# A two-layer vision block on one core: other bands for the second image's convolution, and w_out's tiles seeded and evicted by ScalarE

## The chip, the cores and the metric

The kernel runs on one core of a Trainium2 chip. The metric is the device time of one execution in microseconds. TensorE (PE) multiplies matrices and writes PSUM; VectorE (DVE), ScalarE (ACT) and GpSimd (POOL) work on elements; SyncE (SP) and GpSimd issue DMAs. Each engine runs its own instruction stream in the order in which the program issued it, and the streams meet at semaphores.

## The reference

The input is x of shape (2, 56, 56, 384), in fp32. Layer 0 is neighbourhood attention (12 heads, 7 x 7) and an MLP of 1536 hidden channels. Layer 1 is where the change lies:

```python
h = _layernorm(x, n1_g, n1_b)
p = h @ w_in + b_in                              # 384 -> 768 channels
local = conv 3x3, depthwise, "SAME" (p, k_conv)
lr, rl = _ema_scan(local, axis=2), _ema_scan(local, axis=2, reverse=True)
tb, bt = _ema_scan(local, axis=1), _ema_scan(local, axis=1, reverse=True)
mixed = 0.25 * (lr + rl + tb + bt) + local
mixed = _layernorm(mixed, on_g, on_b)
x = x + (mixed @ w_out + b_out)                  # 768 -> 384
h2 = _layernorm(x, n2_g, n2_b)
return x + gelu(h2 @ w1 + b1) @ w2 + b2          # 384 -> 1536 -> 384
```

An EMA scan is y[t] = 0.6 y[t-1] + 0.4 x[t] along one axis.

## The kernel before

Tokens (pixels) go in groups of four tiles of 128. In time order: attention up to about 600 us; layer 0's MLP, for some groups in a form with seven products for a 2 x 2 block product ("by seven"), for groups g = 5 to 12 in plain form; then layer 1's out projection and MLP, groups ("dgroups") 0 to 2 in plain form up to 1915.6 us, and the rest by seven (the "tail").

A plain group runs 12 hidden blocks m (w1: two times three matmuls each into a bank of PSUM, and GELU by ScalarE, L1208) and then four tiles k of w2 (`tokens`, L1215: 24 matmuls of 384 columns). A layer-0 group is followed by `project_in` of its tokens (w_in), which stores p to DRAM (p_d).

**The convolution beside the matmuls.** Its work is cut into jobs: a `Band` is one image, one block of 128 channels (of six) and a range of rows from BANDS. For one Band: load p's rows (pt), the centre tap (`centre`, on ScalarE if the job is loaded ahead, L1287, else on VectorE, L1289), eight more taps on VectorE (L1304), a scan along the rows both ways (`both_ways`, L1250 to L1254), a product on ScalarE (L1319), and stores of loc and of both to DRAM. When an image's bands are done, `Columns` jobs, one for each block of channels, read loc back turned (`line`, four copies on ScalarE for a half, L1352), scan along the columns, scale the result into "mixed" (L1370, four on ScalarE for a half) and add it to mix_d in DRAM by a DMA that POOL issues (L1323). Band 2 of the second image cannot start before its rows of p are in DRAM.

The steps of these jobs are dealt into the program by class `Beside`: each piece of TensorE work calls `beside.go(worth, own)`, which raises a debt by rate x worth less what VectorE has of its own there, and then issues steps, each with an estimated cost (`us`, and the values yielded by `both_ways`), until the debt is paid. `until(name)` issues all that is left up to a job. So each engine's order is fixed when the program is built: a ScalarE copy that belongs to a Band stands in ScalarE's stream wherever the dealer put it.

**The out projection.** `load_mix(g)` loads a dgroup's "mixed" (mx), and `measure_beside` transposes it (xi, L1440) during m = 3, 5, 7, 9 of the group before, for VectorE's statistics (L221); at m = 10 `close` makes rs, the reciprocal deviation. `project_out(g + 1)` then comes between the 12 blocks of w1 and the four tiles of w2 of group g, four tiles of 12 matmuls; VectorE evicts each with one instruction, product x rs + x (L1485):

```python
nc.vector.scalar_tensor_tensor(
    x3[:, k, :], ps, inner.rs[:, k : k + 1], x[:, k, :], ALU.mult, ALU.add
)
```

`project_out(0)` comes behind the last layer-0 tile of w2, and ahead of it stand that tile's statistics (`norm_w.add`, `close_by_pool`) and `xn = normalized(norm_w, x2, ...)` (four ScalarE instructions, L257). The w2 tiles of a dgroup are seeded: `seeded(res, k)` copies the residual into the PSUM bank by ScalarE (L1225), the matmuls add to it, and ScalarE copies the sum out (L2019). Two seeds are issued before the first w2 tile, each further one after an eviction. `bank()` gives the banks y and y_end in turn; each third tile of the projection takes one of the three banks named pt.

**The switch** to the tail lies in dgroup 2, at k = 2 of w2: `beside.until((1, NI - 1))` ends the convolution, its SBUF pool is closed, the tail's pool is opened in the same space, and VectorE makes sums of w1 and w2 (L1602, L1692). After the last tile POOL makes sums of the tail's input (xsums, L1615).

Of the kernel before, what the change touches and what calls it, by code (L numbers as in the profile page):

```python
# [33 lines left out]
F32 = mybir.dt.float32  # L34
# [27 lines left out]
DECAY, GAIN = 0.6, 0.4  # L62
BANDS = (
    ((0, 28), (28, 47), (47, 56)),
    ((0, 27), (27, 45), (45, 56)),
)
HALF = H // 2
QUARTER = 14
# [45 lines left out]
class Beside:  # L114
# [2 lines left out]

    def __init__(self):
        self.jobs, self.due, self.finished, self.idle = [], 0.0, set(), True
        self.late, self.rate, self.begun = [], 1.04, False  # L120
        self.steps = self.run()

    def behind(self, kind=object):
# [55 lines left out]
def block_kernel(ctx: ExitStack, tc: tile.TileContext, ins: dict, out: bass.AP):  # L179
# [28 lines left out]
    class Norm:  # L208
# [7 lines left out]
        def add(self, k, parts):  # L216

            n = parts[0].shape[0]
            st = self.small.tile([P, 2, 6], F32, name="st")
            for i, x in enumerate(parts):  # L220
                nc.vector.bn_stats(st[:n, i, :], x)  # L221
            nc.vector.bn_aggr(self.mv[:n, k, :], st[:n, : len(parts), :])

        def close(self, k, n=P, first=0):
            rs = self.rs[:n, first:k]
# [868 lines left out]
    def passes(xs, xn, w1, w2, between=lambda ps: None):  # L1094
# [145 lines left out]
        def half(name, tag, bufs=2):  # L1240
            return cp.tile([P, HALF, W], F32, name=name, tag=tag, bufs=bufs)

        def us(lines, each=1.04):

            return 0.2 + lines * W * each / 1000.0

        def both_ways(dst, src):
            n = dst.shape[1]
            d = decay[:, : n * W]
            nc.vector.tensor_tensor_scan(flat(dst), d, flat(src), 0.0, ALU.mult, ALU.add)  # L1250
            end = dst[:, :, W - 1 :]
            nc.vector.scalar_tensor_tensor(end, end, tail - 1.0, end, ALU.mult, ALU.add)
            yield us(n, 2.2) + 0.2
            nc.vector.tensor_tensor_scan(  # L1254
                flat(dst)[:, ::-1], d, flat(dst)[:, ::-1], 0.0, ALU.mult, ALU.add
            )
            yield us(n, 2.2)

        class Band:

# [64 lines left out]
        class Columns:  # L1325
# [32 lines left out]
            def steps(self):  # L1358
# [16 lines left out]
                for c in range(2):  # L1375
                    t = self.lines[c]
                    for step, took in enumerate(both_ways(t, t)):
                        if self.b == 0 and c == step == 0:
                            for h in range(2):
                                mixed.append(half("mixed", "out", 4))  # L1380
                                nc.sync.dma_start(out=flat(mixed[h]), in_=self.rows(mix_d, h))
                        if self.b == 1 and c == 0 and step == 1:
                            self.turn(nc.scalar.copy)
                        yield took
                        if c == 1 and step == 0:
                            behind = beside.behind()
                    for h in range(2):
                        if self.b == 0:
                            to = mixed[h][:, :, c * HALF : (c + 1) * HALF]
                            nc.vector.scalar_tensor_tensor(  # L1390
                                to, t[:, :, h * HALF : (h + 1) * HALF]
                                .rearrange("p w h -> p h w"), share, to, ALU.mult, ALU.add,
                            )
                            if c == 0:
                                self.turn(nc.scalar.copy, (h,))
                            elif h == 1 and isinstance(behind, Columns):
                                behind.turn(nc.scalar.copy, (0,))
                            yield us(HALF / 2, 2.0)
                        else:
                            beside.later(lambda c=c, h=h: turn_back(c, h), 3.0 + 3.5 * c)  # L1400
                    if c == 0:
                        beside.behind()
# [58 lines left out]
        def measure_beside(m, g, ahead):  # L1461


            n = dgroups[g][1]
            k = m // 2 - (1 if g else 2)
            if m == 4:
                add_row(ahead[1], n, "b_out")
            if m == 10 and g:
                ahead[2].close(n)
            if m % 2 == 1 and 0 <= k < n:  # L1470
                measure(ahead[0], ahead[2], k)
                return 2 * STATS
            return 0.0

        def project_out(g, mx, x, inner, then=None):
            n = dgroups[g][1]
            x3 = io.tile([P, NT, C], F32, name="xc")
            norm = Norm(sm)
            for k in range(n):
                third = then is None and k % 3 == 2  # L1480
                ps = tokens(
                    [mx[:, c, :] for c in range(NI)], w_out, k,
                    ps_t.tile([P, C], F32, name="y", tag="pt") if third else None,
                )
                nc.vector.scalar_tensor_tensor(  # L1485
                    x3[:, k, :], ps, inner.rs[:, k : k + 1], x[:, k, :], ALU.mult, ALU.add
                )
                norm.add(k, [x3[:, k, :]])
                if then is not None:
                    then(k)  # L1490
                beside.go(OUT, 2 * STATS)
            norm.close(n)
            return x3, norm
# [108 lines left out]
                engine.tensor_tensor(to, x, y, ALU.subtract)  # L1602
            return *sums, t4, other

        def sums_of_input(hT):

            a, b = slice(0, MT // 2), slice(MT // 2, MT)
            t = tp.tile([P, 4, MT // 2], F32, name="xsums", bufs=1)
            for to, x, y, op in (
                (t[:, 0], hT[:, 0, b], hT[:, 1, b], ALU.add),  # L1610
                (t[:, 1], t[:, 0], hT[:, 0, a], ALU.subtract),
                (t[:, 2], hT[:, 0, a], hT[:, 0, b], ALU.subtract),
                (t[:, 3], hT[:, 1, a], t[:, 1], ALU.subtract),
            ):
                nc.gpsimd.tensor_tensor(to, x, y, op)  # L1615
            return t

        def hidden_by_seven(hT, xsums, w1, w1_sums, s12, measuring, b1):
# [176 lines left out]
        for g, (t0, n) in enumerate(groups):  # L1795
# [19 lines left out]
            if g == last:  # L1815
                beside.until((0, NI - 1))
                load_row(0, "b2_1")
                ahead = load_mix(0)
                beside.rate = 1.06
            if g < last:  # L1820
                x_next, n_next = xs.pop(g + 1), groups[g + 1][1]
                norm_next = Norm(sm) if g < EARLY.stop else Ready(g + 1)
# [89 lines left out]
            if g < last:  # L1912
                add_row(x_next, n_next, "b2_0")
            if g == last:
                ahead[2].close(dgroups[0][1])
                w1, w2_1, w_parts = weights(1)
                for part in w_parts[:3]:
                    part()
# [68 lines left out]
        for g, (t0, n) in enumerate(dgroups[:switch]):  # L1987
# [10 lines left out]
            ahead = load_mix(g + 2)  # L1998
            seeds = [seeded(res, k) for k in range(2)]
            for k in range(n):  # L2000
                if g == switch - 1 and k == 2:

                    beside.until((1, NI - 1))
                    cctx.close()
                    tp = pctx.enter_context(tc.tile_pool(name="tail", bufs=1, reuse_waits="tile"))
                    w1_sums = more_of_w1(w1, three, nc.vector)
                    w2_sums, sum_steps = sums_of_w2(w2, nc.vector)
                if k == n - 1:
                    hT = channels(xn, dgroups[g + 1][1], *n2)
                ps = tokens(hid, w2, k, onto=seeds.pop(0))  # L2010
# [12 lines left out]

        bctx.close()
        ps_y, ps_u, bank_b, banks_b = open_banks(pctx, "tail")
        ps_m = ps_u
        xsums = sums_of_input(hT)
        for step in sum_steps:  # L2030
            step()
        for g, (t0, n) in enumerate(dgroups):
# [136 lines left out]
```

## Time and profile before

| what | value |
|---|---|
| median of 3 runs | 2568.47 us (2565.06 to 2572.3) |
| the profiled execution | 2569.35 us, span 2567.6 us |
| granted TensorE clock, mean | 0.997 |
| TensorE busy | 2532.3 us (99%) |
| VectorE busy | 1986.1 us (77%) |
| ScalarE busy | 1124.0 us (44%) |
| GpSimd busy | 570.3 us (22%) |

The table gives the busy time of each engine over the whole span. Since stages differ, a wait is read in its place: in the windows of the span, in the list of waits, and in the timeline of each engine around it.

### The profile page before, as it was taken

Reading aid. Unit: us, or ns where it says so; the run is one execution under the profiler, and the core shown is the slowest. Engines: PE = TensorE matmul, PEld = TensorE weight load, DVE = VectorE, ACT = ScalarE, POOL = GpSimd, SP = SyncE. Lnnn points to the kernel's source line nnn. Section 1 sums busy time; section 2 is a strip of 40 time slices with the busy share of each in tenths; the row PEclk is TensorE's granted clock in tenths of the full one; section 3 lists DMA queues with packets and bytes.
Section 4 is the critical chain, followed back from the end, with each engine's and each line's share of the span. In section 5 each row is a group of like instructions: output and inputs, shape, how many; then the busy total and the mean of one; then the engine's idle time right before and its main releaser. Section 6 shows DMA issues by size and latency. Waiting matters only on the chain. (4 is left out here: it accounts for less than half of the span.)

```text
span 2567.6 us, 41855 instructions
## 1 busy us (share of the span) xinstructions
PE 2532.3 (99%) x16676; PEld 1733.0 (67%) x16678; DVE 1986.1 (77%) x3715; ACT 1124.0 (44%) x2033; POOL 570.3 (22%) x618
## 2 busy tenths in 40 slices
PE   9999999999999999999999999999999999999999
PEld 5666666666698887455545555554568888888888
DVE  3888878887554453899999996999877877878862
ACT  4656555555443444334555343332862233233222
POOL 0111111111542331010110101011123333333332
PEclk9999999999999999999999999999999999999999
DMA  7432454225522223557687667667781333333210
GB/s 220 152 99 91 148 190 152 90 83 193 168 61 84 68 68 91 167 159 213 179 237 266 214 191 220 202 185 185 203 197 24 75 74 74 74 75 74 47 28 21
DMA packets 155596, 342.96 MB, mean 134 GB/s; under 512 B 11158, under 2 KB 109696, under 8 KB 153088
## 3 DMA queue, kind: packets, MB, share of 16 engines
q1 hardware_dynamic: 124096, 255.65, 29.4%
q0 software_dynamic: 26352, 57.81, 13.3%
q10 hardware_dynamic: 4944, 26.74, 3.0%
q8 instruction: 133, 2.18, 0.4%
q14 instruction: 71, 0.58, 0.1%
HBM read 176.39 MB, written 134.88 MB: 121 GB/s over the span
## 5 line engine op out<-in xcount | busy, mean ns | idle before, releaser
L1304 DVE SCALAR_TENSOR_TENSOR loc<-pt,taps,loc 128x1045 f32<-128x1045 f32 (+17 forms) x288 | 370.6, 1287 | 16.4 <-ACT loc L1287 8.3
L1197 PE MATMUL mm<-hT,w 128*128 128x512 f32 x720 | 319.6, 599 | 0.1
L573 ACT ACTIVATE pts<-pts 119x448 f32<-119x448 f32 (+5 forms) x396 | 210.7, 573 | 107.4 <-DVE pts L563 103.1
L563 DVE TENSOR_TENSOR pts<-sc,bias 119x448 f32<-119x448 f32 (+5 forms) x396 | 219.1, 615 | 45.3 <-PE sc L552 45.0
L1197 PEld LDWEIGHTS mm<-hT,w 128*128 128x128 f32 x720 | 136.0, 192 | 163.0 <-issue 157.6
L1180 DVE STREAM_TRANSPOSE hT<-xn 32x96 f32<-32x96 f32 x784 | 211.3, 269 | 27.7 <-ACT xn L257 17.5
L406 PE MATMUL ps<-hT,wqkv 128*128 128x448 f32 x504 | 206.5, 554 | 2.1 <-ACT vs L451 1.5
L1452 DVE STREAM_TRANSPOSE turned<-mx 32x192 f32<-32x192 f32 x528 | 194.9, 369 | 8.6 <-issue 1.7
L1215 PE MATMUL y_end<-w,hid 128*128 128x384 f32 x552 | 181.9, 486 | 1.4 <-ACT y_end L1225 1.4
L1215 PE MATMUL y<-w,hid 128*128 128x384 f32 x552 | 181.9, 486 | 0.0
L1215 PEld LDWEIGHTS y_end<-w,hid 128*128 128x128 f32 x552 | 104.6, 190 | 73.8 <-ACT y_end L1225 1.7
L1208 ACT ACTIVATE hid<-mm,chan 128x512 f32<-128x512 f32 x120 | 82.1, 685 | 163.4 <-PE mm L1197 163.4
L1215 PEld LDWEIGHTS y<-w,hid 128*128 128x128 f32 x552 | 104.3, 190 | 71.3 <-issue 0.5
L406 PEld LDWEIGHTS ps<-hT,wqkv 128*128 128x128 f32 x504 | 92.0, 191 | 85.3 <-issue 75.5
L1197 PE MATMUL mm<-hT,w_in 128*128 128x512 f32 x324 | 141.9, 596 | 0.6 <-DVE hid_u L1653 0.6
L229 POOL TENSOR_TENSOR rs<-rs,mhalf 128x4 f32<-128x4 f32 (+4 forms) x60 | 57.2, 953 | 312.0 <-DVE rs L226 310.9
L1634 PE MATMUL ua<-hT,w 128*128 128x256 f32 x504 | 122.5, 379 | 0.0
L552 PEld LDWEIGHTS sc<-qT,kT 32*100 32x100 f32 (+3 forms) x3168 | 87.8, 169 | 46.7 <-DVE sum L582 7.6
L1323 POOL DMA_DIRECT2D mix_d<-both x36 | 31.8, 883 | 377.9 <-ACT both L1319 245.8
L592 PE MATMUL o<-pts,vt 100*32 100x112 f32 (+3 forms) x3168 | 115.1, 262 | 0.5 <-ACT pts L573 0.5
L1197 PEld LDWEIGHTS mm<-hT,w_in 128*128 128x128 f32 x324 | 61.7, 192 | 78.3 <-issue 73.3
L1641 ACT ACTIVATE hid<-hid_u,chan 128x256 f32<-128x256 f32 x168 | 76.1, 500 | 82.1 <-DVE hid_u L1653 67.8
(207 smaller groups left out, 4977.6 us busy)
## 6 DMA issues: line engine op xcount, KB each, us to landing
loc<-loc_d SPq DMA_DIRECT2D x24, 784.0 KB
xa<-x_d SPq DMA_DIRECT2D x24, 768.0 KB
xa<-rows POOLq DMA_DIRECT2D x24, 768.0 KB, 11.8
bias<-in_bias_t ACTq DMA_DIRECT2D x13, 1344.0 KB
p_d<-mx SPq DMA_DIRECT2D x11, 1536.0 KB
mx<-mix_d SPq DMA_DIRECT2D x11, 1536.0 KB
v_d<-vs SPq DMA_DIRECT2D x49, 192.0 KB
xr<-in_x SPq DMA_DIRECT2D x49, 192.0 KB
```

The source lines that it names most:

```text
L406: nc.tensor.matmul(ps, lhsT=wqkv[:, c, m * P : (m + 1) * P], rhs=hT[:, c, half_of(n)], start=c == 0, stop=c == NC - 1,)
L552: nc.tensor.matmul(sc[i // 2][: w.keys, i % 2, q : q + TT], lhsT=kT[d, hg, w.keys_at + r * w.kc : w.keys_at + (r + w.rows) * w.kc], rhs=qT ...
L563: nc.vector.tensor_tensor(self.pts[:n, h : h + 2, lo:hi, :], sc[half][:n, :, at * TT : (at + hi - lo) * TT].rearrange("p h (c q) -> p h c ...
L573: nc.scalar.activation(t, t, AF.Exp)
L592: nc.tensor.matmul(o[i * HD : (i + 1) * HD, self.slot, :TT], lhsT=w.vt[:n, c, h * HD : (h + 1) * HD], rhs=self.pts[:n, i, c, :], start=c = ...
L1180: nc.vector.transpose(hT[j : j + HD, :, k * P + i : k * P + i + HD], xn[i : i + HD, k, :].rearrange("p (c q) -> p c q", c=NC)[:, :, j : j ...
L1197: nc.tensor.matmul(ps[:, : n * P], lhsT=w[:, c, m * P : (m + 1) * P], rhs=hT[:, c, : n * P], start=c == 0, stop=c == NC - 1,)
L1208: nc.scalar.activation(t[:, : n * P], ps[:, : n * P], AF.Gelu, bias=col(b1, m))
L1215: nc.tensor.matmul(ps, lhsT=t[:, k * P : (k + 1) * P], rhs=w[:, m, :], start=m == 0 and onto is None, stop=m == len(lhs) - 1, skip_group_c ...
L1304: nc.vector.scalar_tensor_tensor(to, pt[:, lo + dy - self.top : hi + dy - self.top, xt : xt + n], self.tap(dy, dx), to, ALU.mult, ALU.add,)
L1452: nc.vector.transpose(t[j : j + HD].rearrange("p (m c) -> p m c", m=NI)[:, :, i : i + HD], mx[i : i + HD, :, k * P + j : k * P + j + HD],)
L1634: nc.tensor.matmul(bank[:, i, :], lhsT=w[:, m * P : (m + 1) * P], rhs=x, start=start and i == 0, stop=True, skip_group_check=True,)
```

## The change

The second image's bands become 27, 9 and 20 rows instead of 27, 18 and 11. The dealer's estimates become a fixed 0.25 us plus a part by elements, with other values for the scans, and its rate falls from 1.04 to 1.0, and from 1.06 to 0.97 from the last layer-0 group on. For projections of dgroups 0 to 3 (`then is None`) the norm is closed by `close_both_ways`, which also makes sd, the deviation (a further POOL instruction); tiles k = 0, 1 and 3 are seeded with x * sd by ScalarE, the matmuls add to that, and ScalarE evicts with a product by rs, so that rs * (x * sd + product) stands in the place of product * rs + x. Tile 2 stays on VectorE. Two seeds are issued ahead of the projection, the third after tile 0's eviction. The end of the convolution, the closing of its pool and the sums of w1 and w2 move from k = 2 of dgroup 2 to behind its last tile; xsums move from POOL to VectorE, the sums of w2 from VectorE to POOL. The matmuls, the taps' and scans' numbers and the DMAs' kinds stay.

```diff
--- before.py
+++ after.py
@@ -62,7 +62,7 @@
 DECAY, GAIN = 0.6, 0.4
 BANDS = (
     ((0, 28), (28, 47), (47, 56)),
-    ((0, 27), (27, 45), (45, 56)),
+    ((0, 27), (27, 36), (36, 56)),
 )
 HALF = H // 2
 QUARTER = 14
@@ -117,7 +117,7 @@
 
     def __init__(self):
         self.jobs, self.due, self.finished, self.idle = [], 0.0, set(), True
-        self.late, self.rate, self.begun = [], 1.04, False
+        self.late, self.rate, self.begun = [], 1.0, False
         self.steps = self.run()
 
     def behind(self, kind=object):
@@ -220,6 +220,14 @@
             for i, x in enumerate(parts):
                 nc.vector.bn_stats(st[:n, i, :], x)
             nc.vector.bn_aggr(self.mv[:n, k, :], st[:n, : len(parts), :])
+
+        def close_both_ways(self, k):
+
+            self.sd = self.small.tile([P, NT], F32, name="sd")
+            rs, sd = self.rs[:, :k], self.sd[:, :k]
+            nc.vector.scalar_tensor_tensor(sd, self.mv[:, :k, 1], EPS, ones[:, :k], ALU.add, ALU.mult)
+            nc.gpsimd.tensor_tensor(rs, sd, mhalf[:, :k], ALU.pow)
+            nc.gpsimd.tensor_tensor(sd, sd, rs, ALU.mult)
 
         def close(self, k, n=P, first=0):
             rs = self.rs[:n, first:k]
@@ -1240,9 +1248,9 @@
         def half(name, tag, bufs=2):
             return cp.tile([P, HALF, W], F32, name=name, tag=tag, bufs=bufs)
 
-        def us(lines, each=1.04):
-
-            return 0.2 + lines * W * each / 1000.0
+        def us(lines, each=1.04, fixed=0.25):
+
+            return fixed + lines * W * each / 1000.0
 
         def both_ways(dst, src):
             n = dst.shape[1]
@@ -1250,11 +1258,11 @@
             nc.vector.tensor_tensor_scan(flat(dst), d, flat(src), 0.0, ALU.mult, ALU.add)
             end = dst[:, :, W - 1 :]
             nc.vector.scalar_tensor_tensor(end, end, tail - 1.0, end, ALU.mult, ALU.add)
-            yield us(n, 2.2) + 0.2
+            yield us(n, 2.18)
             nc.vector.tensor_tensor_scan(
                 flat(dst)[:, ::-1], d, flat(dst)[:, ::-1], 0.0, ALU.mult, ALU.add
             )
-            yield us(n, 2.2)
+            yield us(n, 2.18, 0.03)
 
         class Band:
 
@@ -1395,7 +1403,7 @@
                                 self.turn(nc.scalar.copy, (h,))
                             elif h == 1 and isinstance(behind, Columns):
                                 behind.turn(nc.scalar.copy, (0,))
-                            yield us(HALF / 2, 2.0)
+                            yield us(HALF / 2, 2.0, 0.0)
                         else:
                             beside.later(lambda c=c, h=h: turn_back(c, h), 3.0 + 3.5 * c)
                     if c == 0:
@@ -1466,7 +1474,7 @@
             if m == 4:
                 add_row(ahead[1], n, "b_out")
             if m == 10 and g:
-                ahead[2].close(n)
+                ahead[2].close_both_ways(n)
             if m % 2 == 1 and 0 <= k < n:
                 measure(ahead[0], ahead[2], k)
                 return 2 * STATS
@@ -1476,12 +1484,26 @@
             n = dgroups[g][1]
             x3 = io.tile([P, NT, C], F32, name="xc")
             norm = Norm(sm)
+            lhs, seeds = [mx[:, c, :] for c in range(NI)], []
+
+            def seed(k):
+                ps = bank()
+                nc.scalar.mul(ps, x[:, k, :], inner.sd[:, k : k + 1])
+                return ps
+
+            if then is None:
+                seeds = [seed(k) for k in range(2)]
             for k in range(n):
-                third = then is None and k % 3 == 2
-                ps = tokens(
-                    [mx[:, c, :] for c in range(NI)], w_out, k,
-                    ps_t.tile([P, C], F32, name="y", tag="pt") if third else None,
-                )
+                if then is None and k != 2:
+                    ps = tokens(lhs, w_out, k, onto=seeds.pop(0))
+                    nc.scalar.mul(x3[:, k, :], ps, inner.rs[:, k : k + 1])
+                    if k == 0 and n > 3:
+                        seeds.append(seed(3))
+                    norm.add(k, [x3[:, k, :]])
+                    beside.go(OUT, STATS)
+                    continue
+                third = ps_t.tile([P, C], F32, name="y", tag="pt") if then is None else None
+                ps = tokens(lhs, w_out, k, third)
                 nc.vector.scalar_tensor_tensor(
                     x3[:, k, :], ps, inner.rs[:, k : k + 1], x[:, k, :], ALU.mult, ALU.add
                 )
@@ -1602,7 +1624,7 @@
                 engine.tensor_tensor(to, x, y, ALU.subtract)
             return *sums, t4, other
 
-        def sums_of_input(hT):
+        def sums_of_input(hT, engine=nc.gpsimd):
 
             a, b = slice(0, MT // 2), slice(MT // 2, MT)
             t = tp.tile([P, 4, MT // 2], F32, name="xsums", bufs=1)
@@ -1612,7 +1634,7 @@
                 (t[:, 2], hT[:, 0, a], hT[:, 0, b], ALU.subtract),
                 (t[:, 3], hT[:, 1, a], t[:, 1], ALU.subtract),
             ):
-                nc.gpsimd.tensor_tensor(to, x, y, op)
+                engine.tensor_tensor(to, x, y, op)
             return t
 
         def hidden_by_seven(hT, xsums, w1, w1_sums, s12, measuring, b1):
@@ -1816,7 +1838,7 @@
                 beside.until((0, NI - 1))
                 load_row(0, "b2_1")
                 ahead = load_mix(0)
-                beside.rate = 1.06
+                beside.rate = 0.97
             if g < last:
                 x_next, n_next = xs.pop(g + 1), groups[g + 1][1]
                 norm_next = Norm(sm) if g < EARLY.stop else Ready(g + 1)
@@ -1912,7 +1934,7 @@
             if g < last:
                 add_row(x_next, n_next, "b2_0")
             if g == last:
-                ahead[2].close(dgroups[0][1])
+                ahead[2].close_both_ways(dgroups[0][1])
                 w1, w2_1, w_parts = weights(1)
                 for part in w_parts[:3]:
                     part()
@@ -1998,13 +2020,6 @@
             ahead = load_mix(g + 2)
             seeds = [seeded(res, k) for k in range(2)]
             for k in range(n):
-                if g == switch - 1 and k == 2:
-
-                    beside.until((1, NI - 1))
-                    cctx.close()
-                    tp = pctx.enter_context(tc.tile_pool(name="tail", bufs=1, reuse_waits="tile"))
-                    w1_sums = more_of_w1(w1, three, nc.vector)
-                    w2_sums, sum_steps = sums_of_w2(w2, nc.vector)
                 if k == n - 1:
                     hT = channels(xn, dgroups[g + 1][1], *n2)
                 ps = tokens(hid, w2, k, onto=seeds.pop(0))
@@ -2023,10 +2038,15 @@
 
 
 
+        beside.until((1, NI - 1))
+        cctx.close()
+        tp = pctx.enter_context(tc.tile_pool(name="tail", bufs=1, reuse_waits="tile"))
         bctx.close()
         ps_y, ps_u, bank_b, banks_b = open_banks(pctx, "tail")
         ps_m = ps_u
-        xsums = sums_of_input(hT)
+        xsums = sums_of_input(hT, nc.vector)
+        w1_sums = more_of_w1(w1, three, nc.vector)
+        w2_sums, sum_steps = sums_of_w2(w2)
         for step in sum_steps:
             step()
         for g, (t0, n) in enumerate(dgroups):
```

## The prediction

> **What bounds the kernel now.** I read the page's busy line first, then the table of stages in windows of 20 us, then the waits of TensorE, then the timelines around each wait.
>
> ```profile
> PE 2532.3 (99%) x16676; PEld 1733.0 (67%) x16678; DVE 1986.1 (77%) x3715; ACT 1124.0 (44%) x2033; POOL 570.3 (22%) x618
> ```
>
> TensorE is busy 99% of the span, so the time is its work plus its gaps. The change leaves its matmuls alone: it can only close gaps, open gaps, or alter the granted clock. The windows (columns: length, PE, PEld, DVE, ACT, POOL busy with counts, granted clock, DMA share, GB/s) say where gaps are:
>
> ```profile
> 1600.00:1620.00 20.00, 20.00 (x64) 11.79 (x63) 14.25 (x15) 2.95 (x5) 0.00 (x0) 1.00 0.33 108
> 1620.00:1640.00 20.00, 16.02 (x55) 9.42 (x54) 19.37 (x26) 5.80 (x8) 2.14 (x3) 0.98 0.45 155
> ...
> 1740.00:1760.00 20.00, 16.78 (x47) 7.70 (x45) 19.30 (x23) 7.20 (x11) 3.18 (x3) 0.97 0.70 160
> 1760.00:1780.00 20.00, 19.05 (x51) 9.31 (x52) 19.17 (x32) 4.73 (x7) 2.50 (x2) 0.86 0.40 133
> 1840.00:1860.00 20.00, 17.44 (x47) 8.20 (x46) 17.92 (x16) 12.38 (x19) 1.75 (x2) 0.91 0.90 210
> ```
>
> Ahead of 1620 PE is full; then come short gaps, with the clock down after them. TensorE's waits from 1600 to 2000 name their owners (total, times, longest):
>
> ```profile
> PE xi L1440 <- DVE st L221: 6.7, 2, 4.2
> PE tp L271 <- DVE xc L1485: 2.5, 1, 2.5
> PE y L1215 <- DVE xc L1485: 1.5, 1, 1.5
> PE y_end L1215 <- ACT y_end L1225: 1.4, 1, 1.4
> ```
>
> That is 12.1 us in all, 10.7 of it owed by VectorE. Why VectorE is late stands in its timeline (start, duration, ..., idle before and its releaser):
>
> ```profile
> 1584.03 0.14 DVE L226 SCALAR_TENSOR_TENSOR rs<-mv,ones 128x4 f32<-128x4 f32 x1
> 1605.40 0.74 DVE L1289 TENSOR_SCALAR loc<-pt,taps 128x1008 f32<-128x1008 f32 x1 [21.23 <-DMA pt<-p_d]
> ```
>
> It stood 21.23 us for image 2's second band, whose rows had not landed, and from then on runs after a schedule it has lost. The gaps end in a slow clock:
>
> ```profile
> 1847.33 0.68 PE L1440 MATMUL xi<-ident,mx 128*128 128x128 f32 x3 [2.56 <-DVE st L221]
> 1847.81 6.92 PE L1197 MATMUL mm<-hT,w 128*128 128x512 f32 x12
> 1855.22 5.32 PE L1197 MATMUL mm<-hT,w 128*128 128x512 f32 x12
> ```
>
> The same 12 matmuls take 6.92 us after a gap of 2.56 and 5.32 us otherwise: 1.6 us lost on top. After the 4.17 us gap at 1760.95 they take 7.33, 2.0 lost; after the 2.48 us gap 36 matmuls take 16.68 where 15.6 is usual, 1.1 lost; after 1.5 us, 0.1. Removable in all: 12.1 + 1.6 + 2.0 + 1.1 + 0.2 = **17 us**.
>
> **The change part by part.**
>
> *Bands, rate, estimates.* A second band of 9 rows needs fewer tokens of project_in, so the 21 us stand goes; what is left between bands is a store and a load, some 2 to 4 us, with no TensorE instruction behind it. The taps, scans and DMAs stay the same in kind: a 504-element tap is about 0.75 us and a 1120-element one 1.41 (line through 616 elements 0.86 and 1008 elements 1.27). The count is the same, 8 taps and two scans for each of three bands. The lower rate pushes the last steps to the last plain tile. I credit this part with all 17 us; bound on the other side: nothing, if VectorE stays late. I take 17, since VectorE's lateness starts at one place and the reason is removed; it also loses 12 evictions of 0.62 us (L1485).
>
> *Seeds and evictions on ScalarE.* In four projections, tiles 0, 1 and 3 get a seed x*sd written to PSUM by ScalarE and are evicted by it. The form is not in the trace; nearest rows are xn L257 (2.50 for four, 0.62 each) and the copy of a seed L1225 (0.48). 0.6 each, 24 of them, 14.4 us on an engine 44% busy: no cost as work. The cost is in the place. An engine's instructions run in program order, so the first matmul of w_out now waits for all that is emitted on ScalarE ahead of its seed. Before, it waited for nothing.
>
> Weighed against that, the Trainium skill ("ScalarE: Activation LUTs", Rules for kernel authors) sends add and mul to VectorE, up to three times faster in bf16. Here, fp32 from PSUM, the rows say 0.62 on both (L257, L1485). By the rule the seeds and evictions would cost ScalarE more than they spare VectorE, and each first seed would come 1.2 us later than by the row (some 5 us more over four projections). I keep the row.
>
> (A) Projection 0 follows the last layer-0 tile of w2. ScalarE first has that tile's normalization, whose chain the trace has, spread over time because VectorE was late:
>
> ```profile
> 1611.57 7.58 PE L1215 MATMUL y_end<-w,hid 128*128 128x384 f32 x23
> ...
> 1619.19 0.48 ACT L1946 COPY xc<-y_end 128x384 f32<-128x384 f32 x1 [6.22 <-PE y_end L1215]
> ...
> 1630.55 0.55 DVE L221 BATCH_NORM_STATS2 st<-xc 128x6 f32<-128x384 f32 x1
> ...
> 1631.68 1.01 POOL L238 TENSOR_TENSOR rs<-rs,mhalf 128x4 f32<-128x4 f32 x1 [43.80 <-DVE off L237]
> ...
> 1633.00 2.50 ACT L257 ACTIVATE xn<-xc,sh,rs 128x384 f32<-128x384 f32 x4 [13.33 <-POOL sh L239]
> ```
>
> From the end of the matmul: eviction 0.04 + 0.48, statistics to POOL 1631.68 - 1630.55 = 1.13 (and 0.1 to get there), POOL to xn 1.32, xn 2.50, seed 0.62 + 0.06 to TensorE: 6.25, and half a tap step in front of the statistics, 0.5: **6.75 us**, in a place where TensorE had no gap. (If VectorE were as late as in this trace, 11 us more: the upper end.)
>
> (B) Projections 1 and 2 follow the last w1 pair. Ahead of the seed: GELU of the last group (0.2 + 0.59) and the centre tap of 1120 elements (1.12 for 1008, so 1.2), then 0.6: **2.6 us each**. Projection 3 has two sets of line copies there, and the trace shows these nearly as they will stand:
>
> ```profile
> 1864.39 3.07 ACT L1352 COPY line<-loc 128x392 f32<-128x392 f32 x4
> 1867.25 0.66 ACT L1208 ACTIVATE hid<-mm,chan 128x512 f32<-128x512 f32 x1
> 1867.81 3.10 ACT L1352 COPY line<-loc 128x392 f32<-128x392 f32 x4
> ...
> 1866.18 4.03 PE L1215 MATMUL y_end<-w_out,mx 128*128 128x384 f32 x12
> ```
>
> ScalarE is done with these at 1870.8, TensorE starts w_out at 1866.18: with 0.62 for the seed, **5.2 us**.
>
> (C) From w_out's last tile to w2. The w2 seed (L1225) came early because VectorE evicted; now it stands behind ScalarE's eviction of tile 3 (0.2 + 0.6), a product of 1120 elements (1.0 to 1.1) and its own 0.48 + 0.06: **2.4 us** in groups 0 and 1; in group 2 four line copies (3.0) instead: **4.35 us**.
>
> *The norm's sd chain.* One more POOL product of 0.20 (as sh L239) behind rs 1.03: done by the seed unless VectorE is 2 us late. Zero, range 0 to 2.
>
> (D) *The switch.* The scans now end in the last plain tile. From the start S of w_out's first tile: w_out 15.5, gap 4.35, w2 31.0, transposes 1.5, so the plain part ends at S + 52.4. VectorE's remaining scans follow ScalarE's line copies (3.0 each) and end about S + 51.5; then mixed x4 (3.15) and its two stores by POOL. Copies into the tail's tiles that lie where "mixed" lay wait for these to land: 8.9 us from issue to landing around the switch (9.6 over the stage). Issue at S + 54.7, landing S + 63.6, copy 0.58, against S + 58.9 when TensorE needs it: **5.3 us**; 3 to 8 by landings of 6.7 to 11.8; 0 if the scans end 5 us sooner. In the trace of before these stores left at 1907.26, 8.4 us before the tail began, and nothing waited. Moving xsums to VectorE costs four short operations (768 elements 0.95; 256 about 0.4) and is hidden behind TensorE's first uz; the w2 sums on POOL (768 elements about 2.2, so 1152 about 3.3, four: 13) have 20 us until they are used.
>
> *Sum.* 6.75 + 2 x 2.6 + 5.2 + 2 x 2.4 + 4.35 + 5.3 = 31.6 us of new gaps. Clock after them, by the rows above: 2.0 for each of A, B3, C3, D, 1.4 for each B of 2.6, 1.1 for each C of 2.4: 13. The Trainium skill ("TensorE: Matmul & The Clock Gate", Part 1) says the clock halves after an idle window of about 3.4 us; by that rule the four gaps under 2.7 us would cost nothing, and 5 us go. The trace has 1.6 lost after 2.56, so the row stands, and the 5 us go into the range. Net: 31.6 + 13 - 17 = +27.6. The profiled execution took 2569.35 (span 2567.6), 0.9 above the median of 2568.47; set against the median: **2595 us**, 1% slower.
>
> **The rivals.**
>
> 1. *Faster: ScalarE is never last.* The seeds would be in PSUM when TensorE arrives, VectorE's 17 us go: 2551.5. It decides where the new waits, with clock, sum to under 17: about 2 us in each of eight places. For it: ScalarE is 44% busy. Against: order, not load; A alone is 8.75, and B3 can be read off the trace. It needs D at nothing and the shorter ones halved. 15%.
> 2. *Smaller waits:* D hidden, clock lost only after gaps over 3.4 us, A without lateness: 26 + 6 - 17, less what ScalarE runs ahead: 2568 to 2581. 17%, of which 8 within 0.3%.
> 3. *The old stalls stay too:* if 9 + 20 rows put VectorE as late as before, nothing is removed: 2612. 8%.
>
> The likeliest is the sum, 60%; over its D and clock bounds 2582 to 2606.
>
> **How the numbers follow.** Slower than 0.3% (7.7 us, about what a measurement here can tell): 60 + 9 + 8 = 77%; within 8%; faster 15%. The range leaves out the first rival and most of the third: 2566 to 2607.
>
> **What would show it.** Right (line numbers of the changed kernel): waits "y or y_end L1223 <- ACT L1491" of 6 to 7, 2.6, 2.6 and 5; of 2.4, 2.4, 4.3 on the w2 seeds (L1233); one on a copy at the tail's ub; a clock under 0.95 in those windows; no more xi waits on st, no 21 us idle on VectorE. Wrong: w_out's first matmuls without a gap, or xi still waiting.

## The result and the profile after

The changed kernel takes 2605.64 us (median of 4 runs, 2603.11 to 2609.13) against 2569.69 for the kernel before in the same comparison: ratio 1.0143, 95% interval [1.0123, 1.0163]. It is 36 us slower. The profiled execution took 2606.84 us (span 2605.0).

The page's busy line of the changed kernel:

```profile
PE 2542.6 (98%) x16678; PEld 1739.1 (67%) x16678; DVE 1976.3 (76%) x3702; ACT 1136.7 (44%) x2058; POOL 584.8 (22%) x622
```

TensorE's work grew by 10 us, the span by 37. The matmuls are the same, so those 10 us are matmuls at a lower clock (mean granted clock 0.991, 0.997 before); the rest is gaps. VectorE lost 10 us of work and ScalarE gained 13, and neither is near full. TensorE's waits from 1580 to 2100 us (total, times, longest):

```profile
PE y L1223 <- ACT y L1491: 11.0, 2, 8.3
PE y_end L1223 <- ACT y_end L1491: 8.9, 2, 4.9
PE ub L1656 <- issue: 8.9, 2, 8.0
PE y L1223 <- ACT y L1233: 6.1, 2, 4.0
PE y_end L1223 <- ACT y_end L1233: 2.1, 1, 2.1
PE xi L1448 <- DVE st L221: 2.0, 1, 2.0
PE mm L1205 <- ACT hT L282: 1.8, 2, 1.2
```

Before, VectorE owed 10.7 us of 12.1. Now ScalarE owes 28.0 through the seeds: 19.9 by the new ones (L1491), 8.2 by w2's (L1233). The xi waits fell from 6.7 to 2.0, and the waits for VectorE's evictions are gone. TensorE's timeline at its gaps in front of w_out and w2, and at the longest one of the tail (start, duration, ..., idle before):

```profile
1627.47 6.64 PE L1223 MATMUL y<-w_out,mx 128*128 128x384 f32 x12 [8.25 <-ACT y L1491]
1705.80 6.73 PE L1223 MATMUL y_end<-w_out,mx 128*128 128x384 f32 x12 [3.96 <-ACT y_end L1491]
1726.22 8.01 PE L1223 MATMUL y<-w,hid 128*128 128x384 f32 x24 [2.08 <-ACT y L1233]
1795.01 5.83 PE L1223 MATMUL y<-w_out,mx 128*128 128x384 f32 x12 [2.71 <-ACT y L1491]
1814.52 8.01 PE L1223 MATMUL y_end<-w,hid 128*128 128x384 f32 x24 [2.08 <-ACT y_end L1233]
1885.54 5.62 PE L1223 MATMUL y_end<-w_out,mx 128*128 128x384 f32 x12 [4.95 <-ACT y_end L1491]
1906.76 10.82 PE L1223 MATMUL y<-w,hid 128*128 128x384 f32 x24 [3.99 <-ACT y L1233]
1956.12 2.05 PE L1656 MATMUL ub<-xsums,w_t 128*128 128x256 f32 x4 [7.96 <-issue]
```

The duration column shows the clock: 12 matmuls of w_out take 4.03 us where no gap stands ahead, and 24 of w2 7.90. Here they take 5.6 to 6.7 and 8.0 to 10.8. The granted clock was 0.74 from 1620 to 1640, 0.83 from 1700 to 1720 and 0.83 from 1900 to 1920.

### The profile page after: what moved, and what is told of

It is laid out like the page before. It is cut to its first block, busy times and chain, and to the rows that moved or that the text cites. A ratio compares the mean times of both kernels' runs of the same rounds, so it can differ in the third digit from the quotient of the medians.

```text
span 2605.0 us, 41875 instructions
## 1 busy us (share of the span) xinstructions
PE 2542.6 (98%) x16678; PEld 1739.1 (67%) x16678; DVE 1976.3 (76%) x3702; ACT 1136.7 (44%) x2058; POOL 584.8 (22%) x622
## 5 line engine op out<-in xcount | busy, mean ns | idle before, releaser
L1312 DVE SCALAR_TENSOR_TENSOR loc<-pt,taps,loc 128x495 f32<-128x495 f32 (+13 forms) x288 | 372.4, 1293 | 39.0 <-ACT loc L1295 22.8
L1460 DVE STREAM_TRANSPOSE turned<-mx 32x192 f32<-32x192 f32 x528 | 194.7, 369 | 13.1 <-issue 6.2
L1223 PE MATMUL y<-w_out,mx 128*128 128x384 f32 x324 | 112.7, 501 | 11.0 <-ACT y L1491 11.0
L237 POOL TENSOR_TENSOR rs<-rs,mhalf 128x4 f32<-128x4 f32 (+4 forms) x56 | 50.2, 897 | 292.3 <-DVE rs L234 291.3
```

The lines of the kernel that those rows point to most:

```text
L1223: nc.tensor.matmul(ps, lhsT=t[:, k * P : (k + 1) * P], rhs=w[:, m, :], start=m == 0 and onto is None, stop=m == len(lhs) - 1, skip_group_c ...
L1312: nc.vector.scalar_tensor_tensor(to, pt[:, lo + dy - self.top : hi + dy - self.top, xt : xt + n], self.tap(dy, dx), to, ALU.mult, ALU.add,)
L1460: nc.vector.transpose(t[j : j + HD].rearrange("p (m c) -> p m c", m=NI)[:, :, i : i + HD], mx[i : i + HD, :, k * P + j : k * P + j + HD],)
```

## The experiments

Each row is compared with the kernel before, run beside it. "Gaps" are TensorE's, in us, from 1600 to the start of the tail and at the switch. They are read from one profiled execution of each kernel, which can lie off the median (2581.2 against 2588.6 for the seeds in another place); the same code ahead of the switch had a gap on hT of 8.8, 8.8 and 7.1 us in the three kernels with a late rate of 1.06 throughout.

| kernel | median us | ratio, 95% interval | gaps up to the tail | gaps at the switch |
|---|---|---|---|---|
| before | 2569.69 | 1 | 12.1 | 0 |
| changed | 2605.64 | 1.0143 [1.0123, 1.0163] | 31.8 | 8.9 |
| VectorE evicts again | 2573.84 | 1.0017 [1.0008, 1.0025] | 0.9 | 16.8 |
| last two stores left out | 2602.03 | 1.0127 [1.0106, 1.0148] | 30.7 | 2.9 |
| seeds in another place | 2588.61 | 1.0066 [1.0045, 1.0087] | 16.2 | 8.3 |
| seeds alone, on before | 2595.48 | 1.0105 [1.0083, 1.0128] | 34.3 | 0 |
| bands alone, on before | 2565.50 | 0.9981 [0.9971, 0.9991] | 7.7 | 2.1 |
| VectorE evicts, old switch, late rate 1.06 | 2573.53 | 1.0015 [1.0008, 1.0022] | 17.9 | 0 |
| VectorE evicts, new switch, late rate 1.06 | 2581.61 | 1.0043 [1.0027, 1.0059] | 17.9 | 5.2 |
| VectorE evicts, old switch, 0.97 then 1.06 | 2563.05 | 0.9972 [0.9962, 0.9982] | 7.9 | 0 |
| the same, 0.97 then 1.10 | 2567.78 | 0.9994 [0.9984, 1.0003] | 13.1 | 0 |
| 0.97 then 1.06, first w2 seed earlier | 2556.32 | 0.9957 [0.9944, 0.9969] | 5.1 | 1.7 |
| 0.97 then 1.04, first w2 seed earlier | 2561.94 | 0.9970 [0.9958, 0.9982] | 3.2 | 3.4 |
| VectorE evicts, new switch, 1.06, w2 sums on VectorE | 2573.62 | 1.0018 [1.0008, 1.0027] | 16.2 | 0 |

**VectorE evicts again.**

```diff
-                ahead[2].close_both_ways(n)
+                ahead[2].close(n)
...
-                if then is None and k != 2:
-                    ps = tokens(lhs, w_out, k, onto=seeds.pop(0))
-                    nc.scalar.mul(x3[:, k, :], ps, inner.rs[:, k : k + 1])
...
+                third = then is None and k % 3 == 2
+                ps = tokens(
+                    [mx[:, c, :] for c in range(NI)], w_out, k,
+                    ps_t.tile([P, C], F32, name="y", tag="pt") if third else None,
+                )
                 nc.vector.scalar_tensor_tensor(
                     x3[:, k, :], ps, inner.rs[:, k : k + 1], x[:, k, :], ALU.mult, ALU.add
                 )
```

> The changed kernel with the projections of dgroups 0 to 3 seeded and evicted as before (VectorE's product x rs + x, close instead of close_both_ways); bands, estimates, rates and the place of the switch stay changed. Theory (place in ScalarE's stream): the seven gaps ahead of w_out and w2 (8.25, 3.96, 2.71, 4.95, 2.08, 2.08, 3.99, sum 28.0 us) go, and with them the slow clock after them (12 matmuls of w_out 6.64, 6.73, 5.83, 5.62 instead of 4.03, 24 of w2 10.82 instead of 7.90: 11.6 us); the gap at the switch (8 us) stays: 2605.6 - 39.6 = 2566 us, or up to 6 more if VectorE, with its 12 evictions back, is late somewhere. Rival (VectorE's new dealing is what is late, the seeds only show it): 2595 to 2606, with the gaps at the evictions or xi.

Measured: 2573.8. All seven seed gaps went; up to 1900 us TensorE has one gap of 0.9. This shows that the seeds cost what they seemed to, and that bands and dealing did remove the old waits. But the kernel is 8 us above the sum expected (2 above its range), for its waits at the tail have grown from 8.9 us to 16.8. Its VectorE timeline has the last scan and the input sums behind it, and its TensorE timeline the two matmul groups that waited:

```profile
1905.83 3.42 DVE L1262 TENSOR_TENSOR_SCAN line<-decay,line 128x1568 f32<-128x1568 f32 x1
1909.29 0.42 DVE L1623 TENSOR_TENSOR xsums<-hT 128x256 f32<-128x256 f32 x1
...
1900.86 1.03 PE L1642 MATMUL ua<-hT,w 128*128 128x256 f32 x4
1909.86 2.04 PE L1642 MATMUL uz<-xsums,w_t 128*128 128x256 f32 x4 [7.98 <-DVE xsums L1623]
1925.95 2.04 PE L1642 MATMUL ub<-xsums,w_t 128*128 128x256 f32 x4 [7.63 <-issue]
```

TensorE began the tail at 1900.86, 8.4 us before the last scan ended. The second wait is for ScalarE's copy into hid_u, which stood until 1925.26 for the landing of the last store into mix_d. In the changed kernel the seed gaps had slowed TensorE so much that the last scan was done at 1941.17, 1.4 us before the tail began (1942.54); taking those gaps away uncovered the next one. The parts of this change do not add.

**The last two stores left out** (image 2, last block of channels; that part of mixed is missing from the sum).

```diff
-                    else:
+                    elif self.m < NI - 1:
                         at = slice(h * HALF * W, (h + 1) * HALF * W)
                         beside.later(
                             lambda h=h, at=at: add_to_mix(self.b, self.m, at, mixed[h]), 11.0
                         )
```

> The changed kernel without the last two stores into mix_d (image 2, last block of channels), so part of the mixed sum is left out. Theory (the tail's copy into hid_u waits for the last store's landing, since its tile lies where mixed lay): the gap of 7.96 us at ub and the slow matmuls after it (2 us) go: 2605.6 - 10 = 2596 us. Rival (the end of the scans, the sums of w1 and w2 or the input sums hold the tail): the gap stays, 2603 to 2606.

Measured: the gap of 7.96 us, in front of the second group of ub matmuls, is gone. Two stand ahead of it, 0.59 and 2.35, where the changed kernel has 0.91, so the switch costs 2.9 instead of 8.9. A line each of POOL and ScalarE in the changed kernel shows the chain that was cut: POOL issues the store, ScalarE's copy waits for it to land, TensorE waits for the copy.

```profile
1944.80 0.87 POOL L1331 DMA_DIRECT2D mix_d<-mixed  x1 [0.49 <-ACT xc L2034]
1955.44 0.58 ACT L1695 COPY hid_u<-ub 128x512 f32<-128x512 f32 x1 [10.20 <-DMA mix_d<-mixed]
```

The median fell by 3.6 us, less than the 10 expected; the intervals of the two ratios overlap, so the gap in the trace is the finding here, not the median. The 2.35 us in front of the first ub group have another owner. One line each of TensorE, ScalarE, VectorE and POOL in the kernel without the stores:

```profile
1942.96 2.04 PE L1656 MATMUL ub<-xsums,w_t 128*128 128x256 f32 x4 [2.35 <-issue]
1938.93 3.13 ACT L1378 ACTIVATE mixed<-line 128x392 f32<-128x392 f32 x4 [4.39 <-DVE line L1262]
1932.84 2.54 DVE L1260 SCALAR_TENSOR_TENSOR line<-line 128x28 f32<-128x28 f32 x1
1931.19 4.11 POOL L1714 TENSOR_TENSOR w_t<-w 128x1152 f32<-128x1152 f32 x1
```

With the store gone POOL began its sums of w2 beside the last scans. VectorE's short operation between two scans ended with POOL's sum and took 2.54 us, where the changed kernel has 0.21; so the last scan, ScalarE's mixed and ub's copy came later. The run thus took out one wait and brought in another.

**The seeds in another place.**

```diff
+        early = [seed_of(ahead[1], ahead[2], k) for k in range(2)]
         xn = normalized(norm_w, x2, groups[g][1])
...
             for m in range(NHID):
+                if m == NHID - 1:
+                    early = [seed_of(ahead[1], ahead[2], k) for k in range(2)]
                 hid.append(hidden(w1, m, hT, n, "L1_conv_b1"))
...
                     nc.scalar.mul(x3[:, k, :], ps, inner.rs[:, k : k + 1])
...
+                    if res is not None and k in (1, 3):
+                        w2_seeds.append(seeded(res, len(w2_seeds)))
```

> The changed kernel with the same ScalarE work in another place: projection 0's two seeds ahead of the normalization, those of projections 1 to 3 ahead of the last GELU of w1, and the two w2 seeds behind the evictions of tiles 1 and 3, ahead of the convolution's ScalarE work. Theory (place, not amount): A from 8.25 to 0, B to 0 to 1.5 (sd's chain), C to 0.7 to 1.4 (own eviction and copy): 2605.6 minus 32 to 38: 2568 to 2574 us. Rival (24 more instructions make ScalarE the bound, or sd's chain does): 2590 or more.

Measured: 2588.6, between the two, but only 1.4 us under the rival's 2590 and 15 above the theory's end. The place is a cause, but this form does not reach what the place alone promised. The same instructions in other places gave back 17 of the 36 us, and the gaps in front of w_out and w2 fell from 28.0 to 8.2. Projection 0's gap fell from 8.25 to 1.06, projection 3's from 4.95 to 1.53, and all three in front of w2 are gone. Two stayed, and a new one came where ScalarE stands 5.3 us for a band's rows (centre tap, L1295) ahead of hT's copies:

```profile
1617.77 4.14 PE L1223 MATMUL y<-w_out,mx 128*128 128x384 f32 x12 [1.06 <-ACT y L1485]
1659.07 12.03 PE L1205 MATMUL mm<-hT,w 128*128 128x512 f32 x24 [6.66 <-ACT hT L282]
1697.05 4.14 PE L1223 MATMUL y_end<-w_out,mx 128*128 128x384 f32 x12 [2.72 <-ACT y_end L1485]
1782.48 4.14 PE L1223 MATMUL y<-w_out,mx 128*128 128x384 f32 x12 [2.92 <-ACT y L1485]
```

So this form has a floor of its own, as the rival said of sd's chain. In projection 1 nothing of the convolution stood ahead of the seed; ScalarE sat idle for sd, the last product of a chain over VectorE and POOL:

```profile
1696.41 0.58 ACT L1485 ACTIVATE y_end<-xa,sd 128x384 f32<-128x384 f32 x1 [3.94 <-POOL sd L230]
```

**The seeds alone, on the kernel before** (`close_both_ways` and the changed `project_out`, with the old bands, rates and switch).

> The kernel before with only the seeds and evictions of ScalarE (close_both_ways and the changed project_out), its own bands, rates and switch. Theory (place): in front of projection 0 TensorE waits for a normalization that ended at 1635.5 while w2 ended at 1619, so about 17 us there; B about 2.5 twice and 5 once, C 2.2 twice and 4 once; clock 10; some 4 us of waits for evictions go: about 2570 + 38 = 2608, 2598 to 2615. Rival (the seeds themselves bring a gain, the bands or the switch cost it): 2555 to 2568.

Measured: 2595.5, slower by 1.05%, 2.5 us below the range that the theory gave and far from the rival's. The main number was met:

```profile
1634.02 6.01 PE L1223 MATMUL y<-w_out,mx 128*128 128x384 f32 x12 [16.82 <-ACT y L1491]
```

17 us was read off the trace of before: w2 ends at 1619, the normalization of a late VectorE ends at 1635.5, and a seed behind it must wait for it. Here VectorE's lateness reaches TensorE in full. Projections 1 and 2 had smaller gaps (1.25, 1.86) than expected: with the old bands and dealing no convolution work stood between the last GELU and the seed in projection 1, and one product of 616 elements (0.71) in projection 2.

**The bands alone, on the kernel before.**

```diff
-    ((0, 27), (27, 45), (45, 56)),
+    ((0, 27), (27, 36), (36, 56)),
```

> The kernel before with the second image's bands of 27, 9 and 20 rows and nothing else. If VectorE's stand of 21 us at the second band is the source of its lateness: the stand falls to a few us, the waits of xi and of the evictions in 1620 to 1860 (10.7 us, with clock 15.5) go or shrink, 2555 to 2562 us. If the old estimates and rates keep VectorE late by themselves: the waits stay, 2566 to 2573.

Measured: 2565.5, 0.2% faster, between the two cases expected. The stand did not shrink, it moved from the second band to the third; VectorE's timeline:

```profile
1677.65 0.80 DVE L1289 TENSOR_SCALAR loc<-pt,taps 128x1120 f32<-128x1120 f32 x1 [21.86 <-DMA pt<-p_d]
```

With the old rate the 9-row band is done before the third band's rows exist. With the late rate 0.97 (VectorE evicts again) VectorE stands 4.75 us there, with 1.06 in its place 14.7 (below). Bands and rate belong together.

**The switch and the late rate.** Two kernels with VectorE's evictions and a late rate of 1.06 in place of 0.97, so that the scans end some two tiles sooner: one has the switch where it was before, one where the change put it.

```diff
-                beside.rate = 0.97
+                beside.rate = 1.06
```

> The changed kernel with VectorE's evictions back, the switch (end of the convolution, sums of w1 and w2, input sums) where and as it was before, and the late rate 1.06 instead of 0.97, so that the last scan is dealt by tile 1 of dgroup 2. Bands, estimates and the early rate 1.0 stay changed. Theory: no gaps before the switch (as in the kernel with the evictions alone put back, under 1 us), none at it: 2569.7 - 17 = 2553 us. If xi waits return with the higher rate: up to 2562. Rival (the new dealing has nothing to give): 2566 to 2572.

> The changed kernel with VectorE's evictions back and the late rate 1.06; the switch stays behind the last plain tile, input sums on VectorE, w2 sums on POOL. If the end of the scans and its stores set the gaps at the switch (8.0 + 1.2 + 7.6 us with the evictions back and rate 0.97): they go with the earlier scans, 2553 to 2558 us. If the moved sums or the closing of the pool set them: the gaps stay, 2568 to 2574.

Measured: 2573.5 and 2581.6, each above every range expected for it. With earlier scans the waits for the last scan and for the last store are gone in both. Both then lose what they should have gained to a gap that the rate makes. In the kernel with the old switch TensorE, ScalarE and VectorE show:

```profile
1665.33 13.52 PE L1205 MATMUL mm<-hT,w 128*128 128x512 f32 x24 [8.78 <-ACT hT L282]
...
1663.98 0.62 ACT L1327 ACTIVATE both<-both 128x504 f32<-128x504 f32 x1 [7.51 <-issue]
1664.52 2.10 ACT L282 ACTIVATE hT<-tp,chan 128x512 f32<-128x512 f32 x3
...
1662.69 1.21 DVE L1262 TENSOR_TENSOR_SCAN both<-decay,both 128x504 f32<-128x504 f32 x1
1678.64 1.08 DVE L1297 TENSOR_SCALAR loc<-pt,taps 128x1120 f32<-128x1120 f32 x1 [14.74 <-DMA pt<-p_d]
```

ScalarE has the second band's last product in front of hT's three copies, and stands for it until VectorE ends that scan at 1663.9; TensorE waits for hT. The trace names no releaser for ScalarE's 7.51 us ("issue"); the scan is the one the product reads, and ends as the product starts. The higher rate put band work in front of hT that VectorE had not done, and VectorE then stood 14.7 us for the third band's rows.

The second kernel has 5.2 us more at the switch, for hid_u from VectorE. Its VectorE and POOL timelines:

```profile
1916.78 3.81 DVE L1623 TENSOR_TENSOR xsums<-hT 128x256 f32<-128x256 f32 x1 [4.88 <-ACT hT L282]
1920.62 2.72 DVE L1623 TENSOR_TENSOR xsums<-xsums,hT 128x256 f32<-128x256 f32 x1
...
1917.10 3.20 POOL L1700 TENSOR_TENSOR w_t<-w 128x1152 f32<-128x1152 f32 x1
1920.38 2.69 POOL L1700 TENSOR_TENSOR w_t<-w,w_t 128x1152 f32<-128x1152 f32 x1
```

Each input sum of VectorE ends 0.3 us behind the POOL sum beside it, and takes 2.7 to 3.8 us instead of 0.42. One more run moved the w2 sums to VectorE:

```diff
-        w2_sums, sum_steps = sums_of_w2(w2)
+        w2_sums, sum_steps = sums_of_w2(w2, nc.vector)
```

> The kernel with VectorE's evictions, the new switch and the late rate 1.06, with the four sums of w2 on VectorE (1.35 us each before) instead of POOL. In the run without this, VectorE's four input sums took 3.81, 2.72, 2.84 and 2.84 us while POOL's sums of w2 ran, against 0.42 in the changed kernel, where they did not overlap. If two-source operations of VectorE and POOL hold each other up: input sums 0.42 to 0.5 each, the 5.2 us wait for hid_u falls below 1.5, 2575 to 2579 us. If the input sums are slow for another reason (their operands): they stay at 3, the wait grows to 8 or more, 2583 to 2588.

Measured: 2573.6, 8 us less by the medians and 6 by the two ratios, 1.4 below the range expected; the input sums take 0.42 and the wait is gone. In the changed kernel the two kinds did not meet: its input sums ended at 1942.8, and POOL began at 1946.3.

**Two late rates.** 0.97 until project_in of the last layer-0 group, then another value from dgroup 0 on.

```diff
+        beside.rate = 1.06
         for g, (t0, n) in enumerate(dgroups[:switch]):
```

> The changed kernel with VectorE's evictions and the switch as before, the late rate 0.97 kept up to project_in of the last layer-0 group, and 1.06 from dgroup 0 on, so that the second band lasts until the third one's rows have landed and the scans still end by tile 1 of dgroup 2. Theory: the 8.8 us gap on hT of the kernel with 1.06 throughout goes (ScalarE's centre tap no longer stands waiting for rows), the switch has its cover back: 2553 to 2560 us. If VectorE cannot keep up with 1.06 there: xi waits of 2 to 4 us come back, 2560 to 2567. Rival (rates make no difference): 2573 as with 1.06 throughout.

> As the run with 1.06 from dgroup 0 on, with 1.10 there. If the switch still waits for scans in the other: this one is faster, 2553 to 2558. If VectorE is at its limit: more xi waits, 2562 to 2570.

Measured: 2563.1 (0.9972 [0.9962, 0.9982]) and 2567.8 (0.9994). The gap on hT is gone in both, and the switch has no gap. With 1.06 two waits are left, xi 5.25 and a w2 seed 2.64: the second of its cases, VectorE not keeping up. With 1.10 the xi waits sum to 10.8. The expectation named the wrong instruction for the gap on hT, a centre tap; it was the product shown above.

**The first w2 seed earlier,** the same copy issued at the projection's last tile, ahead of what is dealt there, on 1.06 and on 1.04.

```diff
                 ps = tokens(
...
                 )
+                if res is not None and k == n - 1:
+                    w2_seeds.append(seeded(res, 0))
```

> As the run with 1.06 from dgroup 0 on, with the first w2 seed (the same ScalarE copy) issued at the projection's last tile, ahead of the convolution's ScalarE work that is dealt there, instead of behind it. If the place in ScalarE's stream makes the 2.64 us gap on y before dgroup 2's w2: it goes with its slow clock (9.70 instead of 7.90): 2563 - 4.4 = 2559 us; the xi gap stays. If not: 2563.

> As that, with 1.04 from dgroup 0 on. If VectorE's share sets the xi gap of 5.25 us in dgroup 1: it shrinks by 2 or more, 2555 to 2558, as long as one half scan more at the switch finds cover. If the switch loses its cover: a gap of 2 to 5 at the tail's ub, 2558 to 2563.

Measured: 2556.3 (0.9957 [0.9944, 0.9969]) and 2561.9. One copy moved in ScalarE's stream closed the 2.64 us gap; by the two ratios it gained 4 us, where 4.4 were expected. All waits of TensorE that are left in the first of them, 1580 to 2050 us:

```profile
PE xi L1448 <- DVE st L221: 5.1, 1, 5.1
PE ub L1644 <- ACT hid_u L1683: 1.7, 1, 1.7
```

It is the fastest kernel of the study, 0.43% below the kernel before (and by the two ratios 1.8% below the changed one), and it holds the bands, the new estimates and not one seed with sd. Its interval overlaps those of the kernels with 1.04 and without the earlier seed, so its rank among these three is not shown. With 1.04 xi fell to 3.2 as expected, and the gap at ub rose to 3.4.

## Why the prediction was right, and where it was off

The forecast was slower, 2595 with 2566 to 2607; measured 2605.6, 1.4 us under the upper end, and one of the four runs (2609.1) lies above it. The direction and the mechanism were right: the seeds stand in ScalarE's order behind work that TensorE had never waited for. That the number stayed inside the range owes something to luck, for nearly all errors of size went the same way. Two slips of the working are small: the sum, set against the median, is 2596 and not 2595, and the line for the taps gives 1.39 us and not 1.41. Of the rows behind the seed's 0.6, L257 works from SBUF and not from PSUM; the seeds took 0.56 to 0.59. Term by term:

- *A, 6.75: measured 8.25.* The mis-sized piece is VectorE's lateness, taken as half a tap step of 0.5. The timelines of ScalarE and VectorE show the eviction done at 1619.74 and its statistics only at 1621.97, behind a scan and two taps; POOL and the normalization then follow as counted:

```profile
1619.26 0.48 ACT L1968 COPY xc<-y_end 128x384 f32<-128x384 f32 x1 [5.96 <-PE y_end L1223]
1624.45 2.50 ACT L265 ACTIVATE xn<-xc,sh,rs 128x384 f32<-128x384 f32 x4 [4.71 <-POOL sh L247]
1626.86 0.56 ACT L1491 ACTIVATE y<-xa,sd 128x384 f32<-128x384 f32 x1
...
1619.44 1.21 DVE L1262 TENSOR_TENSOR_SCAN both<-decay,both 128x504 f32<-128x504 f32 x1
1620.57 1.49 DVE L1312 SCALAR_TENSOR_TENSOR loc<-pt,taps,loc 128x495 f32<-128x495 f32 x2
1621.97 0.56 DVE L221 BATCH_NORM_STATS2 st<-xc 128x6 f32<-128x384 f32 x1
```

- *B, 2.6 twice and 5.2: measured 3.96, 2.71 and 4.95.* The first has 1.49 us on top, for the step that was costed at zero: sd's chain. ScalarE was free and waited for POOL:

```profile
1702.46 1.22 ACT L1295 ACTIVATE loc<-pt,taps 128x1120 f32<-128x1120 f32 x1
1705.17 0.58 ACT L1491 ACTIVATE y_end<-xa,sd 128x384 f32<-128x384 f32 x1 [1.49 <-POOL sd L230]
```

- *C, 2.4 twice and 4.35: measured 2.08, 2.08 and 3.99.* Right to 0.4 us; but the clock stayed at 1.00 in the windows of the two short ones, where below 0.95 was forecast.
- *D, 5.3: measured 8.9.* The copy's gap is 7.96, the upper end of the stated 3 to 8: the landing took 10.6 us from issue (1944.80 to 1955.44) where 8.9 was used, and the store left 59.3 us behind the start of w_out's first tile, not 54.7, while TensorE came to ub only 3.7 us later than reckoned. The other 0.91 came just ahead of it, where ub's copy stood behind the last mixed and an eviction.
- *Clock, 13: measured 13.9.* 2.6 + 2.7 + 1.8 + 1.6 in w_out's first tiles, 2.9 + 0.2 in w2, 2.1 at the tail.
- *Removed, 17: xi kept 2.0 of its 6.7,* and waits on hT came, 1.25 and 0.54, which the kernel before does not have there: 3.8 in all. I had credited the bands with all of the old waits, and put new ones of this kind at nothing.

By these terms: 28.0 + 8.9 + 3.8 of gaps and 13.9 of clock, less 17, is 37.6; the two profiled spans differ by 37.4. The forecast of 27.6 was low by A's and B's lateness (3), D (3.6), the waits on xi and hT (3.8) and the clock (1), less C (1.0) and B3 (0.2).

The first rival, a faster kernel with ScalarE never last, fell: ScalarE is 44% busy and still last in seven places. The two others fell as well: no new gap was hidden, and most of the old ones went. What neither the sum nor a rival had is the cover between parts: with the seeds gone (VectorE evicts again) the switch costs 16.8 us of gaps, not 8.9.

## What to carry to other kernels

An engine with half its time free can still be the last one: before work is moved onto it, list what stands ahead of the moved instruction in its stream and when that is done, for a wait goes into the bound engine at full length and is often followed by a slow clock. An instruction that the bound engine waits for belongs ahead of side work in program order; one copy moved that way was worth a 2.6 us gap here. When a gap is removed, look at what was hidden behind it: work dealt to end "just in time" loses its cover as soon as the bound engine runs faster.

## What the runs showed of the hardware

VectorE was held up by POOL in operations with two sources from SBUF: 128 x 256 sums took 0.42 us alone and 2.7 to 3.8 beside POOL's sums, one for one. POOL's sums took 2.7 to 3.2 us there, about what they take in the changed kernel with no such operation beside them (2.6 to 3.3). In the kernel without the last stores POOL was late too: its first sum began during a scan of VectorE and took 4.11. I had costed the moved sums at nothing by their durations alone. The Trainium skill ("GPSIMD Engine Reference", 1. Specifications) says that the two share SBUF interfaces, with contention for VectorE instructions with two SBUF inputs; the runs agree and show its size.

The clock's loss after a gap does not follow from the gap's length alone. After 2.71 us, 12 matmuls took 5.83 us in the changed kernel; after 2.72 us in the kernel without the last stores they took 4.14, at the same place. After 2.08 us, 24 matmuls took 8.01 in the one and 9.70 in the other:

```profile
1719.50 9.70 PE L1223 MATMUL y<-w,hid 128*128 128x384 f32 x24 [2.08 <-ACT y L1233]
1789.97 4.14 PE L1223 MATMUL y<-w_out,mx 128*128 128x384 f32 x12 [2.72 <-ACT y L1491]
```

These two lines are of the kernel without the last stores, to be held against the third and fourth of the changed kernel's gaps. The Trainium skill ("TensorE: Matmul & The Clock Gate", Part 1) says that the window is free-running, about 3.4 us long. A free-running window fits a loss that depends on where a gap falls. The rule of an idle window, which the prediction cites, would make gaps of 2.08 and 2.71 us cost nothing; here they cost up to 1.8 us, and the measurement decides. Why one of them costs this and another nothing is not shown; the prediction's fixed loss per length is right only in the sum (13 against 13.9).
